# Gram strips of 64 channels, three load buffers in the first half, one pass for both means in the attention, and a product moved ahead of its statistics

## Chip and metric

The kernel runs on one core of a Trainium2 chip. The metric is the device time of one execution in microseconds; before the change its median is 2893.17 us over three runs (2892.83 to 2900.12). The core's engines each work through their own queue in order: PE (TensorE, matrix products; PEld are its weight loads), DVE (VectorE), ACT (ScalarE), POOL (GpSimd) and SP (SyncE, which here only issues DMAs). They meet at semaphores.

## The reference

The input x has the shape (16, 32, 128, 128), float32. Two layers follow each other, each a residual around a group norm and a block. The first is an attention over channels, the second a set of window-wise "FastKAN" blocks. Cut to what matters:

```python
def _gn(v, G=16, eps=1e-5):            # pairs of neighbouring channels
    g = v.reshape(B_, G, C_ // G, H_, W_)
    m = jnp.mean(g, axis=(2, 3, 4), keepdims=True)
    s = jnp.var(g, axis=(2, 3, 4), keepdims=True)
    return ((g - m) / jnp.sqrt(s + eps)).reshape(v.shape)

# layer 0: 8 heads; 8 images together form 256 channels, so there are two halves of the batch
q, k, v = Wq @ t, Wk @ t, Wv @ t                       # t = gn(x), 256 x 16384
attn = softmax(q_h @ k_h.T * 64 ** -0.5)               # 64 x 64 per head
x = x + Wout @ (attn.T-weighted v) + bout

# layer 1, on y = layernorm(windows of gn(x))
def _fastkan(x, ln_g, ln_b, ws, wb, bb):
    ln = _layernorm(x, ln_g, ln_b)
    basis = jnp.exp(-((ln[..., None] - GRID) / DENOM) ** 2)     # 8 grid points
    return flat(basis) @ ws.T + jax.nn.silu(x) @ wb.T + bb
z = fastkan_1(y over rows) + fastkan_2(y over columns) + fastkan_3(y over channels)
x = x + fastkan_4(z) + windows
```

Since queries and keys meet only summed over all 16384 pixels, layer 0 needs of x only the 256 x 256 matrix of its channel products (the Gram matrix) and the channel sums. From these the kernel builds one 256 x 256 matrix per half (`pt`), and layer 0 is then one product of that matrix with x.

## The kernel before

**Stages.** For each half of the batch (`bp` 0 and 1) the Gram loop runs over 16384 pixels: `gram_load` brings 2048 pixels of 256 channels in eight DMAs of 256 KB (four issued by SP, four by ACT) into one of two pairs of tiles (`ad` with `yy`, and two `u`); `gram_turn` turns 512 pixels at a time from channels to pixels on DVE (L653, two transposes a step, into one of two `R` tiles); `gram_sum` adds the products of a step on PE (L676). There are eight loads and 32 steps per half. A step has four blocks of 128 pixels. In a block, the upper triangle of the Gram matrix is made of eight matmuls, each for a strip of 32 channels: in the first bank (`k` = 0) for channels 0 to 127 against all channels from the strip on and a column of ones, in the second for channels 128 to 255. A float32 matmul stands in the profile as two records, each with its own weight load.

`attention(bp)` then turns the Gram matrix into `pt`. It subtracts the rank-one matrix of the channel means (`row_of`, `rank_one`), makes the whole matrix from the triangle with transpositions on PE (`gram_to`, giving the covariance `cov`), derives the group norm's variances, adds the rank-one matrix of the mean's deviations back and repeats `gram_to` scaled by the norm (`gc`). Then come the products with the key weights (L833), the similarity (L848), the softmax, and the products with output and value weights (L874, L883), which give `pt`. From `pt` and `cov` follow the statistics of the second group norm (L908 to L964), stored in `l0c`; after that the key `("layer0", bp)` is set.

Layer 1 works on 64 units of 1024 pixels by 128 channel rows. `layer0_norm` waits for `("layer0", bp)`, makes the product with `pt` (L999) into a PSUM tile of the kind `Y`, and ACT scales it with `l0c` (L1008). The rest of a unit runs through norms, a ladder of 14 long DVE instructions (L1163) and products on PE (L436). Units overlap.

**What sets the order.** All tasks are generators which ask for steps (`step(engine, us, tiles...)`). A planner (`Flow.run`) merges them into one order for each engine, from the costs in the text and the times at which tiles come free; an order of the steady pipeline is written out in `ORDER`, and takes hold once the second Gram sum is found. The engines then keep that order. Tiles of one kind are handed round: `Y` and `X` (PSUM) have two buffers each, `u` six, `ad_r`, `d` and `sd` one each. Until the last similarity, `attention` holds `ad_r`, where its query and key weights lie; `move_back` of a unit needs that tile.

At the start POOL issues 96 small DMAs for parameters (L304 to L308, L501 to L511) and then those of the attention's weights (L598 to L602). DVE prepares the parameters in `parameters`, between the Gram loop's transposes: L572 stands ahead of the transposes of step 20 of the first half, L576 and L577 ahead of those of step 21.

Of the kernel before, what the change touches and what calls it, by code (L numbers as in the profile page):

```python
# [12 lines left out]
ALU = mybir.AluOpType  # L13
# [6 lines left out]
P = 128  # L20
# [219 lines left out]
def conv_preact_kernel(  # L240
# [203 lines left out]
    def layers():  # L444
        with ExitStack() as es:
# [164 lines left out]
            def gram_load():  # L610


                for m in range(NBP * S // LOAD):
                    if m == 0:
                        ad, yy, u0, u1 = yield step("SP", 2.6, "ad", "yy", "u", "u", lag=-2.6)
                        flat4 = lambda t: t.rearrange("p l t w -> p (l t w)")
                        xs = [
                            [t.rearrange("p (g n) -> p g n", g=4) for t in pair]
                            for pair in ((flat4(ad), flat4(yy)), (u0, u1))
                        ]  # L620
                    else:
                        if m >= 2:
                            yield "get", ("turned", 4 * (m - 2) + 3)
                        yield step("SP", 2.6, lag=-2.6)
                    bp, j = divmod(m, S // LOAD)
                    for queue in (nc.sync, nc.scalar):
                        if queue is nc.scalar:
                            yield step("ACT", 2.6)
                        for r in (0, 1) if queue is nc.sync else (2, 3):
                            for k in range(KK):  # L630
                                at = j * LOAD + r * 512
                                queue.dma_start(
                                    out=xs[m % 2][k][32 * r : 32 * r + 32],
                                    in_=x_groups[bp, k, :, :, at : at + 512],
                                )
                    put(("xs", m), xs[m % 2], fl.moved(6.5, 2.6))

            def gram_turn():
# [6 lines left out]
                for m in range(NBP * STEPS):  # L645
                    xr = yield "get", ("xs", m // 4)
                    if m >= 2:
                        yield "get", ("summed", m - 2)
                    yield step("DVE", 1.3)
                    o = slice(128 * (m % 4), 128 * (m % 4) + 128)  # L650
                    for k in range(KK):
                        at = k * (P + 1)
                        nc.vector.transpose(  # L653
                            turned[m % 2][:, :, at : at + P].rearrange("p b (g c) -> p g b c", g=4), xr[k][:, :, o]
                        )
                    put(("turned", m), None)
                    put(("xT", m), turned[m % 2])

            def gram_sum():

                strips = [(0, q, 32 * q, 2 * P + 1) for q in range(4)]
                strips += [(1, q, P, P + 33 + 32 * q) for q in range(3, -1, -1)]
                for m in range(NBP * STEPS):
# [5 lines left out]
                    for b in range(4):  # L671
                        yield step("PE", 0.57, lag=0.0)
                        first, last = i == 0 and b == 0, i == STEPS - 1 and b == 3
                        for k, q, lo, hi in strips:
                            at = k * (P + 1) + 32 * q
                            MM(  # L676
                                g[32 * q : 32 * q + 32, k, lo:hi],
                                lhsT=t[:, b, at : at + 32],
                                rhs=t[:, b, lo:hi],
# [9 lines left out]
            def attention(bp):  # L689
                g_ = yield "get", ("gram", bp)  # L690
                wq, wk, wv_raw, wo, low, mid = yield "get", "projections"
                pt = pts[bp]
                rows = [low[0:1, 512 + i * 256 : 768 + i * 256] for i in range(2)]
                att = mid[:, 1536:1792].rearrange("p (h n) -> p h n", h=PAIRS)
                b_sb = low.rearrange("p (h n) -> p h n", h=PAIRS)
# [31 lines left out]

                def row_of(columns, to):

                    ps_, = yield step("PE", 0.65, "Y")  # L730
                    for k in range(KK):
                        MM(
                            ps_[0:1, 0, k * P : (k + 1) * P],
                            lhsT=columns[:, k : k + 1],
                            rhs=ident,
                            start=True,
                            stop=True,
                        )
                    yield step("DVE", 0.45)
                    nc.vector.tensor_copy(to, ps_[0:1, 0, 0 : KK * P])  # L740
                    give("Y")

                def rank_one(row, scaled, by):
                    yield step("DVE", 0.3)
                    TS(scaled, row, by, None, ALU.mult)
                    ps_, = yield step("PE", 0.9, "Y")
                    for k in range(KK):
                        MM(
                            ps_[:, k, k * P : KK * P],
                            lhsT=scaled[:, k * P : (k + 1) * P],  # L750
                            rhs=row[:, k * P : KK * P],
                            start=True,
                            stop=True,
                        )
                    yield step("DVE", 0.7)
                    for k in range(KK):
                        o = slice(k * P, KK * P)
                        TT(g[:, k, o], g[:, k, o], ps_[:, k, o], ALU.add)
                    give("Y")

                def gram_to(dst, r):

                    yield step("ACT", 0.3, lag=0.0)
                    nc.scalar.copy(parts[:, 2, :], g[:, 0, P : KK * P])
                    yield step("DVE", 0.6)
                    for k, mask in enumerate((upper, lower)):
                        TT(
                            parts[:, k, :].rearrange("p (q c) -> p q c", q=4),
                            g[:, k, k * P : (k + 1) * P].rearrange("p (q c) -> p q c", q=4),
                            mask.unsqueeze(2).to_broadcast([P, 4, 32]),  # L770
                            ALU.mult,
                        )
                    ps_, = yield step("PE", 0.9, "Y")
                    for k in range(KK):
                        to = ps_[:, k, 0:P]
                        MM(to, lhsT=parts[:, k, :], rhs=ident, start=True, stop=False)
                        MM(to, lhsT=ident, rhs=parts[:, k, :], start=False, stop=True)
                    MM(ps_[:, 1, P : 2 * P], lhsT=parts[:, 2, :], rhs=ident, start=True, stop=True)
                    scaled = lambda to, src, k: (
                        nc.vector.tensor_copy(to, src)  # L780
                        if r is None
                        else TS(to, src, r[:, k : k + 1], None, ALU.mult)
                    )
                    yield step("DVE", 1.0)
                    scaled(dst[:, 0, 0:P], ps_[:, 0, 0:P], 0)
                    scaled(dst[:, 0, P:], parts[:, 2, :], 0)
                    scaled(dst[:, 1, 0:P], ps_[:, 1, P : 2 * P], 1)
                    scaled(dst[:, 1, P:], ps_[:, 1, 0:P], 1)
                    give("Y")

                def averaged(matrix, columns, to):
# [14 lines left out]
                give("X", LAG)  # L806
                yield from row_of(mx, rows[0])
                yield from rank_one(rows[0], rows[1], -float(S))
                yield from gram_to(cov, None)


                var, dg, m, d = cols2(), cols2(), cols2(), cols2()
                yield from averaged(pair_n, mx, m)
                yield step("DVE", 1.9)
                for k in range(KK):
                    TT(own, cov[:, k, k * P : (k + 1) * P], ident, ALU.mult)
                    nc.vector.tensor_reduce(dg[:, k : k + 1], own, AX.X, ALU.add)
                TT(d, mx, m, ALU.subtract)
                TT(var, d, d, ALU.mult)
                STT(var, dg, 1.0 / S, var, ALU.mult, ALU.add)  # L820
                gvar = cols2()
                yield from averaged(pair_n, var, gvar)

                yield from row_of(d, rows[0])
                r, _ = yield from rsqrt(gvar)
                yield from rank_one(rows[0], rows[1], float(S))
                yield from gram_to(gc, r)

# [62 lines left out]
                for k in range(KK):  # L891
# [9 lines left out]
                    TT(mine, mine, perm, ALU.add)  # L901
                give("Y")


# [87 lines left out]
            def layer0_norm(n):  # L992
                bp, kk, j = units[n]
                yield "get", ("layer0", bp)
                xr = yield "get", ("x", n // 2)
                xh, xp = yield step("PE", 3.65, "xh", "Y")
                for u in range(2):
                    for k in range(KK):
# [6 lines left out]
                        )  # L1005
                used(("x", n // 2), "x", 2)
                yield step("ACT", 1.06)
                ACT(xh, flat(xp), AF.Identity, bias=l0col(bp, kk, C_XB), scale=l0col(bp, kk, C_R2))  # L1008
# [474 lines left out]
```

## Time and profile before

The profiled execution took 2896.12 us; its span, from the first to the last instruction, is 2894.3 us. All times in the profile are counted from the span's start.

| engine | busy us | share of the span | instructions |
|---|---|---|---|
| PE | 2747.0 | 95% | 48023 |
| PEld | 1085.6 | 38% | 48023 |
| DVE | 2689.1 | 93% | 1811 |
| ACT | 2514.8 | 87% | 2027 |
| POOL | 53.6 | 2% | 109 |

| event | at us |
|---|---|
| first Gram matmul (L676) | 17.1 |
| matmuls of step 20 of the first half | 80.4 |
| DVE clears PSUM for the second half (L669) | 118.6 |
| first product of layer 0 (L999) | 193.5 |
| last Gram matmul record | 235.5 |
| first ladder instruction (L1163) | 250.3 |
| similarity of the second attention (L848) | 302.1 to 305.3 |
| next ladder instruction after it | 324.5 |

A row of the stretches has the stretch (from:to) and its length, then for each engine its busy time and number of instructions, the clock granted to PE (1.00 is full), the share of time in which DMA engines were busy, and GB/s. A row of the waits names who waited for whom, the sum in us, the number of times and the longest. A piece of the chain of waits has its start, its length and the engine, tile and line. In a row of the timeline, start and length come first, then engine, line, operation, tiles and shapes, the number of instructions merged into the row, and in brackets the idle time before it with what ended it. The queue q8 carries instructions to the engine that runs most of them.

### The profile page before, as it was taken

The page shows a single profiled execution, that of the slowest core. Times are in us where ns is not written, and L with a number is a line of the kernel's source. Part 1 is how long each engine was busy: PE and PEld are TensorE (multiplying, and loading weights), DVE is VectorE, ACT ScalarE, POOL GpSimd, SP SyncE. Part 2 cuts the span into 40 slices and gives each one's busy share as a digit, 9 for nine tenths or more (in the row PEclk, how much of TensorE's full clock was granted, in tenths as well). Part 3 has the DMA queues.
Part 4 walks back from the last instruction along what each step waited for, and adds up shares of the span by engine and source line. Part 5 has one row for each costly group of instructions (what it writes and reads, how often), then busy time and mean ns, then how long its engine had stood idle before and what let it go on. Part 6 is the DMA issues. An engine that isn't in the chain of part 4 may idle for free.

```text
span 2894.3 us, 104845 instructions
## 1 busy us (share of the span) xinstructions
PE 2747.0 (95%) x48023; PEld 1085.6 (38%) x48023; DVE 2689.1 (93%) x1811; ACT 2514.8 (87%) x2027; POOL 53.6 (2%) x109
## 2 busy tenths in 40 slices
PE   5798899999999999999999999999999999999985
PEld 5774433333333333333333333333333333333321
DVE  4557699999999999999999999999999999999986
ACT  0018599999999999999999999999999999999973
POOL 6100000000000000000000000000000000000000
PEclk9999899999999999999999999999999999999987
DMA  7751233333333333333333333333333333333311
GB/s 193 187 157 52 67 101 107 116 113 96 106 105 110 114 115 102 112 101 115 113 103 95 109 106 116 114 109 105 107 108 115 107 95 113 100 113 113 103 54 36
DMA packets 206168, 311.31 MB, mean 108 GB/s; under 512 B 24480, under 2 KB 156064, under 8 KB 205728
## 3 DMA queue, kind: packets, MB, share of 16 engines
q1 hardware_dynamic: 192512, 285.29, 33.5%
q10 hardware_dynamic: 9504, 16.85, 2.2%
q8 instruction: 378, 6.19, 0.9%
q0 software_dynamic: 3712, 2.46, 0.4%
q14 instruction: 62, 0.51, 0.1%
HBM read 103.18 MB, written 67.11 MB: 59 GB/s over the span
## 4 chain that ended last, share of the span: by engine, by line
PE 63%; DVE 21%; issue 6%; ACT 5%; DMA 3%; SPq 1%; POOL 1%; DVEq 0%; ACTq 0%; POOLq 0%
PE X L436 25%; DVE u L1163 15%; PE X L1199 10%; PE Y L999 7%; PE Y L436 4%; PE Y L1013 4%; PE X L1318 4%; DVE yc L1134 3%; PE X L676 3%; PE Y L1117 2%; DVE yy L1051 2%; PE Y L976 2%; DMA col<-in_cols 1%; DMA sz<-in_w 1%; SPq L1235 1%
## 5 line engine op out<-in xcount | busy, mean ns | idle before, releaser
L1163 DVE SCALAR_TENSOR_TENSOR u<-R,u 128x2048 f32<-128x2048 f32 x910 | 2043.6, 2286 | 35.4 <-ACT u L1148 17.1
L436 PE MATMUL X<-u,wt_a 32*32 32x512 f32 x16384 | 663.4, 602 | 8.9 <-ACT u L1148 4.2
L436 PE MATMUL X<-u,wt_b 32*32 32x512 f32 x16896 | 637.9, 604 | 16.6 <-ACT u L1148 9.4
L436 PEld LDWEIGHTS X<-u,wt_a 32*32 32x32 f32 x16384 | 301.6, 103 | 287.5 <-issue 136.0
L436 PEld LDWEIGHTS X<-u,wt_b 32*32 32x32 f32 x16896 | 224.1, 103 | 384.0 <-issue 192.4
L1134 DVE TENSOR_TENSOR yc<-yc,Y 128x1024 f32<-128x1024 f32 x260 | 305.4, 1216 | 9.3 <-PE Y L1117 6.7
L1143 ACT ACTIVATE u<-yc,vec 128x2048 f32<-128x2048 f32 x130 | 258.5, 1989 | 30.9 <-DVE yc L1134 26.4
L999 PE MATMUL Y<-x,pt 128*128 128x512 f32 x512 | 236.8, 605 | 33.7 <-DVE yc L1134 33.7
L1109 ACT ACTIVATE yc<-Y 128x1024 f32<-128x1024 f32 x260 | 250.3, 1016 | 13.8 <-PE Y L436 13.8
L1151 ACT ACTIVATE R<-yc,vec 128x2048 f32<-128x2048 f32 x130 | 259.5, 1996 | 2.1 <-DVE u L1163 1.1
L1145 ACT ACTIVATE R<-yc,vec 128x2048 f32<-128x2048 f32 x130 | 258.8, 1990 | 0.0
L1112 ACT ACTIVATE u<-yc 128x2048 f32<-128x2048 f32 x130 | 247.7, 1905 | 3.7 <-DVE u L1163 3.0
L1148 ACT ACTIVATE u<-u 128x2048 f32<-128x2048 f32 x130 | 247.1, 1901 | 0.0
L676 PE MATMUL X<-R 128*32 128x257 f32 (+7 forms) x4096 | 150.2, 303 | 46.8 <-issue 26.3
L978 ACT ACTIVATE lr<-Y,vec 128x512 f32<-128x512 f32 (+1 forms) x194 | 131.5, 678 | 46.2 <-PE Y L976 41.9
L676 PEld LDWEIGHTS X<-R 128*32 128x32 f32 x4096 | 136.0, 115 | 66.3 <-issue 36.4
L999 PEld LDWEIGHTS Y<-x,pt 128*128 128x128 f32 x512 | 92.0, 189 | 182.6 <-issue 92.6
L976 PE MATMUL Y<-u,e 128*32 128x512 f32 x1040 | 139.6, 604 | 3.4 <-ACT u L1112 3.4
L1227 ACT ACTIVATE ad<-X,col 128x1024 f32<-128x1024 f32 x128 | 134.0, 1096 | 0.1
L1013 PE MATMUL Y<-xh,c 128*128 128x512 f32 x256 | 127.0, 618 | 1.3 <-DVE yc L1134 1.3
L979 ACT ACTIVATE lr<-lr 128x512 f32<-128x512 f32 (+1 forms) x194 | 122.3, 631 | 6.1
L1199 PE MATMUL X<-sd,silu_a 64*64 64x512 f32 x1024 | 124.7, 602 | 0.0
(202 smaller groups left out, 2486.5 us busy)
## 6 DMA issues: line engine op xcount, KB each, us to landing
xh<-xh SPq DMA_DIRECT2D x128, 512.0 KB
d<-yy SPq DMA_DIRECT2D x512, 128.0 KB
ad_r<-ad SPq DMA_DIRECT2D x512, 128.0 KB
x<-in_x SPq DMA_DIRECT2D x32, 1024.0 KB
out<-xh SPq DMA_DIRECT2D x256, 128.0 KB
u<-in_x SPq DMA_DIRECT2D x32, 256.0 KB
u<-in_x ACTq DMA_DIRECT2D x32, 256.0 KB
ad<-in_x SPq DMA_DIRECT2D x16, 256.0 KB
```

Source lines behind the costliest of these rows:

```text
L436: MM(dst(to, g_), lhsT=wt[32 * g_ : 32 * g_ + 32, :], rhs=rhs(g_, (to - turn[g_]) % 4), start=start, stop=stop,)
L676: MM(g[32 * q : 32 * q + 32, k, lo:hi], lhsT=t[:, b, at : at + 32], rhs=t[:, b, lo:hi], start=first, stop=last,)
L999: MM(xp[:, u, :], lhsT=pts[bp][:, k, kk * P : (kk + 1) * P], rhs=xr[:, k, u * 512 : (u + 1) * 512], start=k == 0, stop=k == KK - 1,)
L1109: ACT(v[:, i * RB : (i + 1) * RB], flat(yt[i]), AF.Identity)
L1112: ACT(sq, v, AF.Square)
L1134: TT(v[:, o], v[:, o], flat(rb[i]), ALU.mult)
L1143: ACT(u, v, AF.Square, bias=bq)
L1145: ACT(up, v, AF.Exp, bias=bp_, scale=2.0)
L1148: ACT(u, u, AF.Exp, scale=-1.0)
L1151: ACT(down, v, AF.Exp, bias=bn, scale=-2.0)
L1163: STT(t, by, BIG, tiles[at[way]], ALU.min, ALU.mult)
L1199: MM(dst(i, f), lhsT=wt(i)[o, o], rhs=rhs(i, o), start=False, stop=False)
```

## The change

In `gram_load`, a third pair of tiles (`d` with `sd`) takes part in the first half's loads, in turn with the two others; `gram_turn` gives it back after the last step of that half. In `gram_sum`, strips are 64 channels wide, four matmuls a block in place of eight. In `attention`, the rows of the channel means and of the mean's deviations are made together, the two rank-one matrices in one PSUM tile, the transposition is done once (for `cov`), and `gc` is the sum of `cov` and the second rank-one matrix, scaled afterwards; several copies go to ACT. `layer0_norm` waits for a new key `("matrix", bp)`, which is set when `pt` is there, makes its product, and waits for `("layer0", bp)` only ahead of the scaling on ACT. The helpers `row_of`, `rank_one` and `gram_to` go.

```diff
@@ gram_load
-                for m in range(NBP * S // LOAD):
+                half = S // LOAD
+                turn = [m % 3 if m < half else m % 2 for m in range(NBP * half)]
+                for m in range(NBP * half):
                     if m == 0:
-                        ad, yy, u0, u1 = yield step("SP", 2.6, "ad", "yy", "u", "u", lag=-2.6)
+                        ad, yy, u0, u1, d, sd = yield step("SP", 2.6, "ad", "yy", "u", "u", "d", "sd", lag=-2.6)
...
-                            for pair in ((flat4(ad), flat4(yy)), (u0, u1))
+                            for pair in ((flat4(ad), flat4(yy)), (u0, u1), (flat4(d), flat4(sd)))
...
-                        if m >= 2:
-                            yield "get", ("turned", 4 * (m - 2) + 3)
+                        old = [i for i in range(m) if turn[i] == turn[m]]
+                        if old:
+                            yield "get", ("turned", 4 * old[-1] + 3)
...
@@ gram_turn
+                    if m == STEPS - 1:
+                        give("d")
+                        give("sd")
@@ gram_sum
-                strips = [(0, q, 32 * q, 2 * P + 1) for q in range(4)]
-                strips += [(1, q, P, P + 33 + 32 * q) for q in range(3, -1, -1)]
+                strips = [(0, q, 64 * q, 2 * P + 1) for q in range(2)]
+                strips += [(1, q, P, P + 65 + 64 * q) for q in range(1, -1, -1)]
...
-                            at = k * (P + 1) + 32 * q
+                            at = k * (P + 1) + 64 * q
                             MM(
-                                g[32 * q : 32 * q + 32, k, lo:hi],
-                                lhsT=t[:, b, at : at + 32],
+                                g[64 * q : 64 * q + 64, k, lo:hi],
+                                lhsT=t[:, b, at : at + 64],
                                 rhs=t[:, b, lo:hi],
@@ attention
-                yield from row_of(mx, rows[0])
-                yield from rank_one(rows[0], rows[1], -float(S))
-                yield from gram_to(cov, None)
                 var, dg, m, d = cols2(), cols2(), cols2(), cols2()
                 yield from averaged(pair_n, mx, m)
-                yield step("DVE", 1.9)
+                yield step("DVE", 0.2)
+                TT(d, mx, m, ALU.subtract)
+                ps_, = yield step("PE", 1.0, "Y")
+                for i, columns in enumerate((mx, d)):
+                    for k in range(KK):
+                        MM(ps_[0:1, i, k * P : (k + 1) * P], lhsT=columns[:, k : k + 1], rhs=ident, ...)
+                yield step("ACT", 0.55, lag=0.0)
+                for i in range(2):
+                    nc.scalar.copy(rows[i], ps_[0:1, i, 0 : KK * P])
+                yield step("DVE", 0.8)
+                for i in range(2):
+                    TS(scaled[i], ps_[0:1, i, 0 : KK * P], float(S) if i else -float(S), None, ALU.mult)
+                give("Y")
+                ps_, = yield step("PE", 1.7, "Y")
+                for i in range(2):
+                    for k in range(KK):
+                        o = slice(0 if i else k * P, KK * P)
+                        MM(ps_[:, k, i * KK * P + o.start : (i + 1) * KK * P],
+                           lhsT=scaled[i][:, k * P : (k + 1) * P], rhs=rows[i][:, o], ...)
+                yield step("DVE", 0.7)
+                for k in range(KK):
+                    o = slice(k * P, KK * P)
+                    TT(g[:, k, o], g[:, k, o], ps_[:, k, o], ALU.add)
+                yield step("ACT", 0.9, lag=0.0)
+                nc.scalar.copy(parts[:, 2, :], g[:, 0, P : KK * P])
+                nc.scalar.copy(gc, ps_[:, :, KK * P :])
+                give("Y", LAG)
...
+                yield step("ACT", 0.5, lag=0.0)
+                nc.scalar.copy(cov[:, 1, 0:P], ps_[:, 1, P : 2 * P])
+                nc.scalar.copy(cov[:, 0, P:], parts[:, 2, :])
+                yield step("DVE", 2.3)
+                nc.vector.tensor_copy(cov[:, 0, 0:P], ps_[:, 0, 0:P])
+                nc.vector.tensor_copy(cov[:, 1, P:], ps_[:, 1, 0:P])
...
-                yield from row_of(d, rows[0])
+                TT(gc, gc, cov, ALU.add)
+                give("Y")
                 r, _ = yield from rsqrt(gvar)
-                yield from rank_one(rows[0], rows[1], float(S))
-                yield from gram_to(gc, r)
+                yield step("DVE", 0.5)
+                for k in range(KK):
+                    TS(gc[:, k, :], gc[:, k, :], r[:, k : k + 1], None, ALU.mult)
...
                     TT(mine, mine, perm, ALU.add)
                 give("Y")
+                put(("matrix", bp), None, LAG)
@@ layer0_norm
-                yield "get", ("layer0", bp)
+                yield "get", ("matrix", bp)
                 xr = yield "get", ("x", n // 2)
                 xh, xp = yield step("PE", 3.65, "xh", "Y")
...
                 used(("x", n // 2), "x", 2)
+                yield "get", ("layer0", bp)
                 yield step("ACT", 1.06)
```

## The prediction

> **What bounds the kernel now.** I read the stretches first, cut where the work changes: start, first half of the Gram loop up to a stop of VectorE, its rest, second half, start of the layer-1 pipeline, steady pipeline.
>
> ```profile
> core 0: us, PE busy (x) PEld busy (x) DVE busy (x) ACT busy (x) POOL busy (x), PEclk, DMA share, GB/s
> 17.10:80.40 63.30, 47.88 (x1287) 43.88 (x1288) 34.19 (x89) 0.00 (x0) 42.18 (x85) 0.92 0.73 180
> 80.40:118.70 38.30, 29.02 (x768) 26.68 (x768) 18.03 (x29) 0.00 (x0) 2.49 (x3) 0.87 0.82 216
> 118.70:235.60 116.90, 111.13 (x2320) 88.47 (x2312) 64.11 (x150) 23.29 (x30) 0.00 (x0) 0.97 0.56 149
> 235.60:305.30 69.70, 57.82 (x741) 22.66 (x736) 59.25 (x71) 52.80 (x44) 0.00 (x0) 0.98 0.08 24
> 400.00:2800.00 2400.00, 2355.46 (x40512) 852.25 (x40504) 2365.28 (x1324) 2328.65 (x1867) 0.00 (x0) 1.00 0.36 107
> ```
>
> From 400 us on, PE, DVE and ACT are all busy 97 to 99%. The change touches none of that work, and in the instruction order of the two programs each engine runs the same steps there. So the question is how much earlier the pipeline starts; a microsecond gained before 400 us is a microsecond of the span. PE sets the second Gram half (111.1 of 116.9 us busy). In the first half it idles 15.4 + 9.3 us, and the waits of PE from 17.2 to 118.7 us name the cause (17.1 us of the second row is the start):
>
> ```profile
> PE X L676 <- issue: 22.5, 9, 4.2
> PE X L676 <- DVE R L653: 19.3, 4, 17.1
> ```
>
> "Issue" is a wait for nothing the profile shows. The chain of waits shows two limits there, one after the other:
>
> ```profile
> 65.23 7.30 DMA sz<-in_w
> ...
> 75.80 4.55 DMA sz<-in_w
> 80.49 0.25 DVE sz L576
> ...
> 81.56 0.64 DVE R L653
> ...
> 85.22 4.20 PE X L676 x75
> 89.42 4.19 issue
> ...
> 100.63 8.18 PE X L676 x152
> 108.81 3.11 issue
> ```
>
> Up to 81.5 us the chain is POOL's row of small parameter loads: VectorE takes its queue in order, and the parameter steps (L572 ahead of the transposes of step 20, L576 ahead of those of step 21) wait for the last of them. After it, PE with holes of 3 to 4 us.
>
> **The holes are late instructions.** PE runs 48023 matmul and as many weight-load instructions; queue q8 moved 6.19 MB in 378 packets, which is 64 B for each and 256 in a packet. One Gram step (512 pixels, 32 matmuls of two records) is 128 instructions, so a packet lasts two steps, 4.4 us. Asked in slices of 1 us, q8 moved a packet in those that begin at 45, 58, 71, 82 and 109 us, each at the end of a 2 MB burst of x, and PE resumed at 48.5, 60.9, 73.7, 85.2 and 111.9, some 2.5 us later each time. From the start of one packet's work to that of the next took 7 to 8.4 us there (85.22 to 93.61 the longest), against 4.4 us of work.
>
> The Trainium skill, "Runtime: NRT & Kernel Launch", section "Instruction fetch mechanics", agrees on 256 instructions, but calls the fetch hidden by the rate of issue, with 2048 instructions held for PE. By that rule the holes are something else, and the term of 9.3 us below would be nothing. The rows of q8 decide against it.
>
> **Strips of 64.** Removed: 16 of the 32 matmuls of a step, 64 of its 128 instructions. Columns: the four 32-wide strips stream 1160 columns side by side in four column strips, 290 each; the two 64-wide ones 644 in two, 322 each.
>
> ```profile
> 66.19 2.18 PE L676 MATMUL X<-R 128*32 128x257 f32 x64
> 193.50 3.70 PE L999 MATMUL Y<-x,pt 128*128 128x512 f32 x8
> 157.79 1.20 PE L848 MATMUL Y<-att,ad_r 128*64 128x64 f32 x32
> ```
>
> Now 2.18 us a step. L999 streams 8 x 512 columns in 3.65 us (its piece in the chain of waits; 3.70 with its tail), 0.89 ns a column; 322 x 2 records x 4 blocks at that rate is 2.30 us, the lower bound. Scaling the present step by 322/290 gives 2.42, the upper. L848 has 64-wide strips and shows that two overlap: 32 x 64 columns one by one would be 1.82 us, it took 1.20. I take 2.35: +0.17 a step. A packet now lasts 9.4 us, over the longest fetch seen (8.4), so I take the holes as gone.
>
> **Three load buffers.** No load is added. The first half's eight loads go out up to one buffer earlier; SyncE and ScalarE issue the same DMAs in the same places, and ScalarE has no other work until 118 us. VectorE's waits for x loads after the first one sum to 2.6 us up to 118 us (rows of the waits: 2.2 and 0.4), so the direct gain is nothing. What it costs: the bursts close up, and POOL's parameter loads run among them. From 36.5 to 76.8 us POOL issued 56, about 1.2 per us inside a burst and 1.75 between. PE without holes does step 18 by 17.1 + 18 x 2.35 = 59 us and then stands on the same in-order parameter steps; loads stand with it, as their buffers do not come free, and POOL regains the quiet rate. From 37 to 58 us at 1.2 per us, 25 are issued; then one more burst of 8 us (10) and 21 at 1.75 end at 78, and with 4.5 of landing the last is usable at 82.5, against 80.4 to 81.5 now: +1. Bounds: 96 issues of 0.5 us never waiting end near 50 + 4 us, and then PE itself sets the end (17.1 + 32 x 2.35 = 92, 26 us earlier than 118.7); all at the busy rate, 56/1.2 from 37 on, end at 84 + 8, 10 later. I take +1, as both ends correct themselves.
>
> So the first half's saving of 20 steps dies in the wait for parameters. What counts is its last 12 steps: now 38.3 us, 29.0 busy (26.2 at 2.18, the rest at a granted clock of 0.87 after each hole) and 9.3 idle. After: 12 x 2.35 = 28.2, with 1.5 for one slow restart 29.7. First half: 29.7 - 38.3 + 1 = -7.6 us.
>
> **Second half.** PE is the limit: 32 x 0.17 = +5.4; issue waits there were 3.9 us in 3 holes, taken as gone; attention's PE work see next, -1.5. Together 0, bounds -3 to +6.
>
> **Attention in one pass.** Removed for each half: the second row-of-columns, rank-one and transposition passes. Three of the eleven PE trips between the Gram sum and the similarity go. PE work: one transposition set (1.6 us) less, one 256-column rank-one product more (0.1 to 0.2), -1.5. Added: ACT copies (0.3 to 0.5 us each; ACT idles 94 of 117 us in the second half), one DVE add, one scaling. In the first attention the trips lie under Gram steps on PE, so only the 1.5 counts. The second runs among the pipeline's first unit; from 235.6 to the similarity (L848, 302 to 305.3) PE idles 11.9 us. Three of eleven trips are 3 us of it, with 1.5 of work 4.5; I take -4. Bounds 0 (the idle time belongs to the pipeline filling) and -13 (all of it). What follows does not shrink: the similarity still releases ad_r, whose move (5.1 us of issues plus 4 of landing) and the softmax still hold PE and DVE until some 19 us later, as now (305.3 to 324.5).
>
> **Product before the group norm's statistics.** L999 of unit 0 (3.65 us) moves about six Gram steps forward in PE's order. PE is saturated, so its sum is unchanged; it holds one of two Y buffers while the statistics chain, serial anyway, uses the other. ACT's L1008 still waits for l0c. Next product and transposes behind it stand at the same Gram steps as before. Nothing; if PE had been idle there, 3.65 us would be won.
>
> **Sum.** -7.6 + 0 - 4 = -11.6. The profiled execution took 2896.12 us (span 2894.3); the median is 2893.17. So 2893.2 - 11.6 = 2881.6, said as 2881.
>
> **Rivals.**
> 1. *Parameters stop binding* (POOL done by 65 to 70 us): -26 instead of -7.6 at most; halfway, -17 - 4: 2872, at best 2863. For: the quiet gaps were real. Against: 96 issues and the waits of the chain.
> 2. *Same*: a step of 2.42 (+0.07 x 44 = +3), parameters 4 us later, pipeline start gains nothing: -11.6 + 3 + 3 + 4 = -1.6, 2891. For: L848 has 36 ns a record, more than L676's 34. Against: these must fall together.
> 3. *Slower*: 64-wide strips cost much more because the two column strips do not run side by side as four do, at L676 in the saturated stretch. Price 44 steps x (c - 2.35). Decides at c = 2.61 (no gain) and is beyond 0.3% slower at 2.82; wholly one by one, c = 4.6, +99 - 12: 2980; a quarter of that overlap lost, 2.9, gives +24 - 12: 2906, which I take as its time. For: no row shows strips of this shape with unequal widths. Against: L848.
> 4. *The fetch is not it*: holes stay (9.3 + 3.9): 2894.8. It falls into rivals 2 and 3.
>
> **Chances.** Forecast (2872 to 2886) 0.45, rival 1 0.15, rivals 2 and 4 (2886 to 2899) 0.25, rival 3 0.15. 0.3% is 8.7 us, about what a measurement here can tell from none: below 2884.5 lie 0.43 of the forecast and rival 1, 0.58; above 2901.9 rival 3 and a tail, 0.17; the rest 0.25. For 8 in 10 I cut 2863 below and 2896 above.
>
> **What would show it.** Right: no issue holes of 3 us in the Gram stretch, half of q8's packets there; PE waiting for R (DVE) some 15 to 20 us ahead of step 20 or 21, and that step at 81 to 83 us; the X memset of the second half near 111 instead of 118.6; second half as long as before; L848 of the second attention some 65 us after the last Gram matmul. Wrong: steps over 2.6 us, holes that stay, or a start of step 21 far from 82 us.

## The result, and the profile after

The changed kernel takes 2882.26 us (median of seven runs, 2881.65 to 2886.40), the kernel before 2893.66 us (2892.83 to 2904.04) beside it, so the medians differ by 11.4 us. The ratio of their fast runs is 0.9947, with a 95% interval of 0.9936 to 0.9957, which would be 12 to 19 us. The two agree only roughly; the gain is best taken as 11 to 15 us. The profiled execution took 2885.47 us; its span is 2883.7 us against 2894.3.

The total came out as forecast (2881, that is -11.6 us). The parts did not. The account below takes marks from the timelines of the two profiled executions; a unit is marked by DVE's product in its norm (`yy<-xc,Y`), and the 17th ladder instruction is the first one behind the second attention's similarity before, at 324.5 us.

| stretch | before, us | after, us | difference | predicted |
|---|---|---|---|---|
| start to first Gram matmul | 17.1 | 17.2 | 0.0 | 0 |
| to the matmuls of step 20 | 63.3 | 72.5 | +9.3 | +1 |
| last 12 steps, to the clearing of PSUM | 38.2 | 28.5 | -9.6 | -8.6 |
| second half, to the last Gram record's end | 117.1 | 116.0 | -1.1 | 0 |
| from there to the 17th ladder instruction | 88.8 | 79.5 | -9.4 | -4 |
| to the norm of unit 4 | 64.8 | 68.7 | +4.0 | 0 |
| unit 4 to unit 63 | 2341.6 | 2338.4 | -3.2 | 0 |
| to the end | 163.5 | 162.9 | -0.6 | 0 |

Each column is one execution, and the first half scatters. Two kernels below, with only the attention or only the key changed, run the same instructions there in the same order as the kernel before; they started step 20 at 84.7 and 84.2 us, not 80.4, and their first half took 99.1 and 97.1 us, not 101.4. Against them the +9.3 would be 5 to 6 and the -9.6 only -2 to -3.

The first half's own gain was lost again; the attention gave 5.4 us net; and 3 us more appear in the steady pipeline, where nothing was changed. All fourteen profiled executions here, whose DVE and ACT run the same steps there, lie between 2338.4 and 2341.7 us, so those 3 us are scatter of which this pair shows the two ends.

The waits of PE in the first half of the kernel after (17.2 to 118.5 us: who waited for whom, sum, times, longest):

```profile
PE X L683 <- DVE R L657: 38.2, 7, 17.2
```

The "issue" row, 22.5 us before, is gone: PE now waits for the transposes alone (17.2 us of the row is the start, so 21.0). Also gone are half of q8's packets between 17 and 118 us, first before, then after (packets, MB, share):

```profile
q8 instruction: 15, 0.25, 1.1%
q8 instruction: 8, 0.13, 0.6%
```

The stretches of the kernel after, cut where the work changes (first Gram matmul, step 20, clearing, last Gram matmul, similarity):

```profile
core 0: us, PE busy (x) PEld busy (x) DVE busy (x) ACT busy (x) POOL busy (x), PEclk, DMA share, GB/s
17.10:89.70 72.60, 51.49 (x643) 47.73 (x643) 34.24 (x91) 0.00 (x0) 41.72 (x85) 0.89 0.94 208
89.70:118.50 28.80, 28.78 (x383) 27.38 (x383) 18.07 (x29) 0.00 (x0) 3.02 (x4) 0.91 0.61 153
118.50:234.20 115.70, 114.39 (x1287) 92.08 (x1284) 63.73 (x142) 27.44 (x35) 0.00 (x0) 0.99 0.57 150
234.20:295.40 61.20, 53.61 (x724) 20.33 (x722) 51.99 (x60) 49.48 (x46) 0.00 (x0) 0.97 0.09 27
```

From step 20 on PE is full (28.78 of 28.80). Ahead of it PE idles 21.1 us, 5.7 more than before. The chain of waits of the kernel after says for what:

```profile
57.29 7.42 DMA sz<-in_w
...
64.99 6.71 DMA sz<-in_w
...
77.22 7.29 DMA wt_b<-in_w
...
85.83 1.80 DMA sz<-in_w
...
88.17 0.70 DVE R L657
...
89.72 26.78 PE X L683 x261
...
118.25 0.92 DVE X L676
```

It is the same row of parameter loads as before, only that its last load goes out at 86 us and not at 76. What DVE waited for in that half, on the same columns:

```profile
DVE wt_b L572 <- DMA sz<-in_w: 11.4, 1, 11.4
DVE sz L550 <- DMA sz<-in_w: 10.7, 2, 8.4
```

Each of these waits stands ahead of transposes in DVE's order, and PE stands behind those. The step itself is read off the transposes that wait for PE's `R`, in the saturated stretch of the kernel after:

```profile
107.72 1.52 DVE L657 STREAM_TRANSPOSE R<-u 128x512 f32<-128x512 f32 x2 [0.67 <-PE X L683]
109.92 1.53 DVE L657 STREAM_TRANSPOSE R<-u 128x512 f32<-128x512 f32 x2 [0.68 <-PE X L683]
112.12 1.53 DVE L657 STREAM_TRANSPOSE R<-u 128x512 f32<-128x512 f32 x2 [0.67 <-PE X L683]
```

One step every 2.20 us, against 2.18 with strips of 32, as long as PE has only Gram steps to do. In the second half other products lie between the steps, and there the Gram records alone kept PE busy for 3 us more than before, as these two rows show (stretch, length, PE's busy time on the products of `R`, clock, DMA share, GB/s; before, then after):

```profile
118.57:235.66 117.09, 74.16 (x2059) 0.97 0.56 149
118.25:234.25 116.00, 77.22 (x1032) 0.99 0.57 151
```

Over the five executions with strips of 32 that time is 72.0 to 74.2 us; in the kernel with the strips of 64 alone it is 78.0. So a step costs 0.1 to 0.2 us more there.

Back to the first half: its last twelve steps took 28.5 us; 12 x 2.20 is 26.4, and 2.1 went to the restart: PE began at a granted clock of 0.52, as two stretches of 5 us show.

```profile
90.00:95.00 5.00, 5.00 (x42) 4.55 (x42) 2.67 (x7) 0.00 (x0) 1.45 (x3) 0.52 1.01 215
95.00:100.00 5.00, 5.00 (x79) 4.86 (x75) 3.05 (x5) 0.00 (x0) 1.22 (x1) 1.00 0.51 101
```

The second attention, from the timeline of the kernel after:

```profile
294.16 1.20 PE L851 MATMUL Y<-att,ad_r 128*64 128x64 f32 x32 [0.70 <-DVE yc L1139]
...
298.15 2.28 DVE L1168 SCALAR_TENSOR_TENSOR u<-R,u 128x2048 f32<-128x2048 f32 x1
313.71 2.28 DVE L1168 SCALAR_TENSOR_TENSOR u<-R,u 128x2048 f32<-128x2048 f32 x1
318.07 9.28 DVE L1168 SCALAR_TENSOR_TENSOR u<-R,u 128x2048 f32<-128x2048 f32 x4 [0.47 <-PE X L436]
```

The similarity ends 61.1 us after the last Gram record (69.6 before), and the 17th ladder instruction starts at 313.71, 18.3 us behind it (19.2 before). Then 4.0 us of these 9.4 are given back: from that instruction to the norm of unit 4 DVE was busy 59.3 of 64.8 us before and 60.1 of 68.7 after. It now waits for ACT, which waits for PE's products of a unit; the waits of DVE in the kernel after from 313.7 to 382.4 us begin so:

```profile
DVE u L1168 <- ACT yc L1114: 3.4, 1, 3.4
```

### The profile page after: what moved, and what is told of

Its sections match the earlier page's. It is cut to its first block, busy times and chain, and to the rows that moved or that the text cites. A ratio compares the mean times of both kernels' runs of the same rounds, so it can differ in the third digit from the quotient of the medians.

```text
span 2883.7 us, 100690 instructions
## 1 busy us (share of the span) xinstructions
PE 2748.3 (95%) x45955; PEld 1092.4 (38%) x45955; DVE 2685.2 (93%) x1793; ACT 2518.4 (87%) x2035; POOL 53.8 (2%) x109
## 4 chain that ended last, share of the span: by engine, by line
PE 64%; DVE 21%; issue 6%; DMA 4%; ACT 3%; SPq 1%; DVEq 0%; POOL 0%; ACTq 0%; POOLq 0%
PE X L436 25%; DVE u L1168 15%; PE X L1204 10%; PE Y L1003 8%; PE Y L1018 4%; PE Y L436 4%; PE X L1323 4%; PE X L683 3%; DVE yc L1139 3%; PE Y L980 2%; PE Y L1122 2%; DVE yy L1056 2%; DMA sz<-in_w 1%; DMA col<-in_cols 1%; SPq L1240 1%
## 5 line engine op out<-in xcount | busy, mean ns | idle before, releaser
L683 PE MATMUL X<-R 128*64 128x193 f32 (+3 forms) x2048 | 156.7, 313 | 39.0 <-DVE R L657 38.2
L683 PEld LDWEIGHTS X<-R 128*64 128x64 f32 x2048 | 145.1, 142 | 56.7 <-DVE R L657 40.8
```

The lines of the kernel that those rows point to most:

```text
L683: MM(g[64 * q : 64 * q + 64, k, lo:hi], lhsT=t[:, b, at : at + 64], rhs=t[:, b, lo:hi], start=first, stop=last,)
```

## Experiments

Each kernel ran against the kernel before on the same chip. The interval of a ratio reaches 0.1 to 0.2% to either side, 3 to 5 us; the marks in a profile are finer, but are one execution. Two stretches are used: the first half, from the first Gram matmul to DVE's clearing of PSUM (101.4 us before, 101.1 after), and what follows it, from the clearing to the norm of unit 4 (270.7 before, 264.2 after). The kernel before took 2895 to 2897 us beside these runs, so ratios are compared, not times.

### The four parts one by one

Strips alone, in the kernel before:

```diff
-                strips = [(0, q, 32 * q, 2 * P + 1) for q in range(4)]
-                strips += [(1, q, P, P + 33 + 32 * q) for q in range(3, -1, -1)]
+                strips = [(0, q, 64 * q, 2 * P + 1) for q in range(2)]
+                strips += [(1, q, P, P + 65 + 64 * q) for q in range(1, -1, -1)]
...
```

> Before with 64-channel strips alone: two load buffers, attention and product as before. Theory A (late instruction packets make the holes): PE has no issue wait of 3 us left in the Gram stretch; as the third buffer is not there to crowd POOL's loads, step 20 still starts at 80 to 83 us, the second half starts near 109 instead of 118.6, and the time is 2880 to 2886. Theory B (the holes are something else, the gain came from the attention): holes stay, second half starts at 117 to 119, time 2891 to 2895.

2884.37 us, ratio 0.9953 [0.9942, 0.9965]. The waits of PE in its first half:

```profile
PE X L676 <- DVE R L653: 29.4, 3, 16.8
```

No wait for "issue" is left, the first half takes 90.9 us, and what follows it is unchanged (271.5). Step 20 started at 78.7 us, a little ahead of the 80 to 83 expected. So the strips alone bring 10.5 us in the first half, more than the 7.6 that the prediction gave to the whole change there, and far more than the whole change got.

The third load buffer alone:

```diff
+                turn = [m % 3 if m < half else m % 2 for m in range(NBP * half)]
...
-                            for pair in ((flat4(ad), flat4(yy)), (u0, u1))
+                            for pair in ((flat4(ad), flat4(yy)), (u0, u1), (flat4(d), flat4(sd)))
```

> Before with three load buffers in the first half alone. Theory A (closed-up loads slow POOL's parameter loads, and the parameters gate step 20): step 20 starts at 86 to 91 us instead of 80.4, holes of PE stay in the steps before it, the second half starts at 117 to 123, time 2892 to 2898. Theory B (the buffer costs nothing and the parameters moved late for another reason): step 20 at 80 to 83 us, time 2885 to 2893.

2898.24 us, ratio 1.0001 [0.9993, 1.001]. The waits of PE in its first half:

```profile
PE X L683 <- DVE R L657: 27.3, 3, 17.8
PE X L683 <- issue: 15.6, 6, 4.5
```

The holes stay, and step 20 starts at 87.1 us, as theory A said; but the second half starts at 114.5 us, ahead of its range, since PE had one hole of 1.8 us in the steps behind it. Over the whole kernel the buffer alone neither helps nor harms.

The attention in one pass alone (the change's edits in `attention`, without the new key):

```diff
-                yield from row_of(mx, rows[0])
-                yield from rank_one(rows[0], rows[1], -float(S))
-                yield from gram_to(cov, None)
...
+                for i, columns in enumerate((mx, d)):
...
-                yield from gram_to(gc, r)
```

> Before with the one-pass attention alone. Theory A (fewer PE trips bring the second similarity, L848, forward among the pipeline's first unit): first half as before (second half starts at 118 to 119.5), similarity ends 8 to 10 us earlier after the last Gram matmul than the 70 us of before, of which about 4 are given back by the next unit; time 2883 to 2888. Theory B (only its 1.5 us of PE work counts): 2890 to 2892.5.

2885.69 us, ratio 0.996 [0.9947, 0.9973]. The holes stay here too (15.3 us in 7), and what follows the first half takes 267.1 us, 3.6 less than before. The similarity ended 65.0 us after the last Gram record, 4.7 earlier than before and not the 8 to 10 expected. The first half, in which the same instructions run as before, took 99.1 us instead of 101.4; that is scatter, here and in the next run.

The key alone:

```diff
+                put(("matrix", bp), None, LAG)
...
-                yield "get", ("layer0", bp)
+                yield "get", ("matrix", bp)
...
+                yield "get", ("layer0", bp)
                 yield step("ACT", 1.06)
```

> Before with the product of layer 0 waiting for the matrix alone, not for the norm's statistics. Theory A (PE is saturated there, a step moved within its queue changes nothing): last Gram matmul at 234.5 to 236.5 us, time 2891 to 2895. Theory B (the product was on the path): 3 to 4 us less, 2889 to 2890.5.

2890.49 us, ratio 0.9976 [0.9964, 0.9988]; at 2893 for the kernel before that is 2886, below the range of either theory. Its profile gives 4.3 us to the first half, whose instructions up to there are those of the kernel before, and 2.3 to what follows. This could not tell whether the moved product is worth anything; the last experiment below asks again.

### What the third buffer does beside the strips

The changed kernel with two load buffers, as in the kernel before (the second diff above taken back):

> The changed kernel with two load buffers in the first half as before (strips, attention and product as changed). Theory A (the third buffer crowds POOL's parameter loads and gives the strips' gain back): step 20 starts at 79 to 83 us instead of 89.7, the second half starts at 107 to 110 instead of 118.3, the rest as in the changed kernel; ratio to before 0.990 to 0.993, 2.5 to 10 us below the changed kernel. Theory B (the third buffer does not matter): second half at 116 to 119, ratio 0.994 to 0.996.

2871.77 us, ratio 0.9913 [0.9899, 0.9926]: faster than the whole change, whose interval is 0.9936 to 0.9957. Its first half takes 90.1 us. The stretches of this kernel up to the wait for parameters:

```profile
17.00:37.00 20.00, 19.70 (x250) 18.91 (x252) 11.52 (x17) 0.00 (x0) 13.41 (x27) 1.00 0.83 210
37.00:57.00 20.00, 20.00 (x280) 18.48 (x278) 14.56 (x41) 0.00 (x0) 12.95 (x27) 1.00 0.95 244
57.00:65.00 8.00, 6.12 (x90) 5.73 (x84) 5.25 (x29) 0.00 (x0) 4.78 (x10) 1.00 0.57 136
```

And the same stretches of the changed kernel, with three:

```profile
17.00:37.00 20.00, 19.82 (x246) 18.89 (x247) 10.69 (x16) 0.00 (x0) 10.52 (x21) 1.00 1.08 229
37.00:57.00 20.00, 19.07 (x261) 17.59 (x259) 14.27 (x40) 0.00 (x0) 9.46 (x20) 1.00 1.07 231
57.00:65.00 8.00, 5.77 (x81) 5.23 (x79) 4.51 (x17) 0.00 (x0) 4.01 (x9) 1.00 1.07 239
```

PE does nearly the same in both. The column to read is POOL's number: 27 + 27 + 10 = 64 issues with two buffers, 21 + 20 + 9 = 50 with three. With three the DMA engines have no gap (share 1.07 to 1.08 throughout), so that POOL's small loads land later (the 4.5 KB ones after 7.3 us in the median, 6.3 with two) and POOL, which waits for some of them, issues about one per us instead of 1.3. The 14 issues that are missing cost some 10 us behind: the last load of the row goes out at 75 us with two buffers, at 86 with three. In ratios, strips, attention and key alone add up to 1.1% less time, the three together with two buffers give 0.87%, and with the third buffer 0.53% is left.

### The wait for parameters itself

The changed kernel (three buffers), with all parameter steps of DVE that stood between the Gram loop's transposes held until the first half's last step is turned:

```diff
+                yield "get", ("turned", STEPS - 1)
                 yield step("DVE", 0.6)
                 nc.vector.memset(back_t, 0.0)
```

> The changed kernel with the parameter steps of VectorE and PE moved behind the first half's Gram steps. Theory A (the parameters are the gate of the first half): PE runs all 32 steps without a wait for R over 1 us, the second half starts at 89 to 93 us instead of 118.3; attention may then wait for its own weights until 100; ratio 0.982 to 0.988. Theory B (something else, as the loads of x, holds the first half): second half at 105 or later, ratio over 0.990.

2862.32 us, ratio 0.9881 [0.9864, 0.9898]. Its first half as one stretch:

```profile
16.80:91.20 74.40, 73.53 (x1024) 70.00 (x1024) 46.22 (x75) 0.27 (x1) 41.44 (x84) 1.00 1.03 236
```

74.4 us for 32 steps, PE busy for 73.5 of them at the full clock. The parameters end 17 us later than in the changed kernel (107.5 against 90.3 us), and nobody waits for them there: what follows the first half takes 266.1 us, about as after.

The same edit with two buffers:

> As the run with late parameters, but with two load buffers. Theory A (a load takes about 8 us of the 8.8 that four steps last, so two buffers leave small waits for R at each load, which the third hides): second half starts at 93 to 100 us, ratio 0.984 to 0.990, behind the three buffers. Theory B (the third buffer only takes bandwidth from the parameters): second half as early or earlier than with three.

2866.09 us, ratio 0.9888 [0.9872, 0.9904]; first half 78.9 us. The second half starts at 95.7 us, in theory A's range, but not by its mechanism. PE runs all 32 steps in 72.5 us with no wait for `R`; the time goes behind them, where DVE waits for the second half's first load, and its clearing of PSUM (L670) stands behind those transposes:

```profile
16.75 72.45 PE L677 MATMUL X<-R 128*64 128x257 f32 x1024 [16.75 <-DVE R L654]
...
90.51 0.71 DVE L654 STREAM_TRANSPOSE R<-ad 128x512 f32<-128x512 f32 x1 [3.81 <-DMA ad<-in_x]
94.17 0.71 DVE L654 STREAM_TRANSPOSE R<-yy 128x512 f32<-128x512 f32 x1 [2.94 <-DMA yy<-in_x]
```

Once the parameters are out of the way, the third buffer does no harm, and at most brings the 3 to 4.5 us that the stretch up to the clearing is shorter with it; the totals' intervals overlap.

### Number of instructions, or their shape

The changed kernel with strips of 32 (the first diff taken back):

> The changed kernel with strips of 32 channels. Theory A (late instructions): issue waits of 3 to 4.5 us are back in the Gram stretch, before and after the parameters; step 20 again at 85 to 91 us, second half starts at 116 to 123; ratio 0.996 to 0.999. Theory B (strips do not matter): as the changed kernel, 0.994 to 0.995.

2886.8 us, ratio 0.9968 [0.9958, 0.9979]; first half 97.7 us. The waits of PE in it:

```profile
PE X L683 <- DVE R L657: 25.1, 3, 18.3
PE X L683 <- issue: 14.1, 7, 3.7
```

The holes are back. This does not tell the number of instructions from the width, so the next kernel keeps the strips of 64 and fills up the number:

```diff
                                 rhs=t[:, b, lo:hi],
...
+                            if bp == 0:
+                                MM(
+                                    spare[64 * q : 64 * q + 64, k, 0:1],
+                                    lhsT=t[:, b, at : at + 64],
+                                    rhs=t[:, b, 0:1],
...
```

> The changed kernel, but in the first half each strip's matmul is followed by one more of a single column into a second X tile, whose result nobody reads: 128 instructions a step again, with the 64-wide strips kept. Theory A (the holes come from the number of instructions: a packet of 256 lasts two steps): issue waits of PE of 1.5 to 4.5 us return in the first half, 8 to 20 us in 5 to 9 waits, and the packets of q8 there double. Theory B (a 32-wide shape makes the holes, not the number): no issue wait over 1 us, as in the changed kernel. The time says little by itself, since each extra matmul costs work on PE: step between 2.3 and 3.3 us, total 2880 to 2905 on the scale where the kernel before has 2893.

2911.17 us, ratio 1.0052 [1.0037, 1.0067]. The waits of PE in its first half, which is now PE's own 113.7 us long (3.55 a step):

```profile
PE X L685 <- DVE R L657: 17.5, 1, 17.5
PE X L693 <- issue: 3.9, 3, 2.5
PE X L685 <- issue: 1.4, 2, 1.2
```

Waits for "issue" return, 14 packets of q8 are back between 17 and 118 us, and the longest wait, 2.5 us, is too long for the theory of the shape. The three longest end each 2.5 to 2.8 us after a packet of q8 started (at 29.96, 38.98 and 98.65 us), as in the kernel before:

```profile
32.79 0.16 PE L693 MATMUL X<-R 128*64 128x1 f32 x1 [1.24 <-issue]
41.73 0.17 PE L693 MATMUL X<-R 128*64 128x1 f32 x1 [2.49 <-issue]
101.17 0.33 PE L685 MATMUL X<-R 128*64 128x65 f32 x2 [1.16 <-issue]
```

But the sum is 5.3 us, not the 8 to 20 expected: the extra matmuls make a step so long (the 2.3 to 3.3 expected are exceeded too) that a packet lasts 7.1 us, which most fetches stay under. So the number decides, together with the time that a packet lasts: 4.4 us a packet gives 14 to 22 us of holes, 7.1 us gives 5, and 8.8 us (four steps of 2.20) none.

### The next limit, and the product

On top of late parameters, the first load of layer 1's `x`, 1 MB that SP issues ahead of the Gram loads, is held until step 7 is turned:

```diff
+                if n == 0:
+                    yield "get", ("turned", 7)
                 bp, kk, j = units[n]
                 xr, = yield step("SP", 1.6, "x")
```

> Late parameters as before, and the first load of layer 1's x (unit 0, 1 MB, issued ahead of the Gram loads) is held until step 7 of the first half is turned. Theory A (the first Gram load waits behind that megabyte on the DMA engines): first Gram matmul 2.5 to 5 us earlier than 16.8, everything after it as much earlier, ratio 0.9865 to 0.9875 against 0.988 with late parameters alone. Theory B (the start is set by latency and code, not by bytes): first Gram matmul within 1 us of 16.8, ratio as with late parameters alone.

2860.39 us, ratio 0.9877 [0.9862, 0.9892]. PE's timeline in its first half:

```profile
14.79 19.63 PE L684 MATMUL X<-R 128*64 128x257 f32 x256 [14.79 <-DVE R L658]
34.63 9.01 PE L684 MATMUL X<-R 128*64 128x257 f32 x128 [0.22 <-DVE R L658]
43.89 9.01 PE L684 MATMUL X<-R 128*64 128x257 f32 x128 [0.24 <-DVE R L658]
55.51 37.07 PE L684 MATMUL X<-R 128*64 128x257 f32 x512 [2.61 <-DVE R L658]
```

The start moves 2.0 us forward, between the two theories, though clear of the 16.8 to 18.3 us of all other executions here: the megabyte costs something, less than said. At 53 us 2.6 us are lost again, as DVE waits 2.6 us for a load of x there; the first half takes 79.0 us and ends 2.6 us later than in the first execution of late parameters alone, 1.2 later than in the one below. So the gain was nothing. That the first half is by now about as long as its loads (DMA share 1.00 to 1.03) would explain it; no run tested that.

Late parameters once more, beside it:

> The kernel with late parameters once more, beside the one above on the same chip. Ratio 0.987 to 0.989; first Gram matmul at 16.8, clearing of PSUM for the second half at 91 to 92 us.

2860.82 us, ratio 0.9877 [0.986, 0.9893]; clearing at 92.6 us, what follows 268.7. Between this execution and the first of the same kernel that stretch differs by 2.7 us.

Late parameters, with layer 0's product again behind the statistics:

```diff
-                put(("matrix", bp), None, LAG)
...
-                yield "get", ("matrix", bp)
+                yield "get", ("layer0", bp)
                 xr = yield "get", ("x", n // 2)
...
-                yield "get", ("layer0", bp)
                 yield step("ACT", 1.06)
```

> Late parameters as before, but layer 0's product again behind the statistics of the second group norm, as in the kernel before. Theory A (the moved product is worth nothing): ratio as with late parameters, 0.987 to 0.989, and from the clearing of PSUM for the second half to the norm of unit 4 as long as there, 266 to 269 us. Theory B (it is worth the 2 to 7 us that the key alone seemed to bring): ratio 0.9895 to 0.991, that stretch 269 to 273 us.

2862.21 us, ratio 0.9886 [0.9868, 0.9903]; what follows the first half takes 267.4 us, between the 266.1 and 268.7 us of the same kernel with the product moved. The stretch speaks for no gain. The ratios' intervals, some 5 us to either side, would not rule out the 2 to 7 us either; what the key alone seemed to bring is not seen again here, and not excluded.

The fastest versions are those with late parameters, 1.2% below the kernel before and some 0.7% below the changed one.

## Why the prediction held, and where it did not

**The holes and the fetch.** Right. Strips alone take them away, fillers bring some of them back with the shape kept. Rival 4 falls with that. The Trainium skill, "Runtime: NRT & Kernel Launch", section "Instruction fetch mechanics", calls the fetch of the next 256 instructions hidden by the rate of issue; here it was not, as long as a packet lasted 4.4 us and the x loads ran beside it.

**The step.** Taken at 2.35 us with a lower bound of 2.30; it is 2.20. The bound was wrong where PE has only Gram steps: it took 0.89 ns a column from L999, and 2.20 us over 2 x 4 x 322 columns are 0.85. With half as many instructions the step hardly grew there, +0.02 where +0.17 was said. Among the other products of the second half it grew by 0.1 to 0.2, as said. That two strips of 64 run side by side well enough was right, and rival 3 falls.

**The wait for parameters.** This is the term that was mis-sized: +1 us was said, +9.3 measured, near the upper bound of 10 (5 to 6 against the two other executions of the same first half). The step that failed is the sentence that PE "then stands on the same in-order parameter steps; loads stand with it" and "POOL regains the quiet rate" from 66 us or so. The slower rate began earlier, not at 37 us but with the Gram loop (21 issues from 17 to 37 us against 25 before), and it lasted longer, as a third buffer lets one more load of 2 MB go out (issued from 57.7 to 64.5 us): the DMA engines were full until 70 us. The rate inside the bursts, 1.2 per us, was also read too high, about 1.0 with no gaps. "Both ends correct themselves" held for neither.

**The last twelve steps.** -9.6 against -8.6: 12 x (2.35 - 2.20) = 1.8 us better in the step, 0.6 worse in the restart (2.1 for 1.5).

**The second half.** 0 was said, -1.1 came, as the terms changed about as said in sum: the Gram records added 3.1 us (+5.4 said), the transpositions that went took off 3.1 (-1.5 said), and PE's idle time fell by 4.5, from 5.8 to 1.3, with the waits for "issue" (3.9) gone. What was not said: records of the units behind worth 3.9 us moved ahead of the last Gram record.

**Attention.** -4 against -5.4 net (-9.4 and +4.0). Over the runs with the one pass, what follows the first half took 261 to 269 us (275 with the fillers), without it 268 to 274; on average 265.6 without the fillers, and 271.1. The working was less good than its sum: PE's idle time up to the similarity fell by 4.3 us and its work there by 4.2, where 3 and 1.5 were said; "what follows does not shrink" held up to the next ladder (18.3 for 19.2 us), but the pipeline behind it gave 4.0 us back to a wait for products, which was not foreseen. PE's records tell what the 4.2 us are: its transpositions there went from 28 records to 18 (8.0 to 5.0 us), and six records of other units (3.7 us) moved ahead of the last Gram record, while some others took longer.

**The moved product.** Nothing was said, and nothing is seen beside late parameters, within some 5 us.

**The third buffer.** "The direct gain is nothing" was right as long as the parameters bind; its cost beside the strips is the 10 us that the wait for parameters took. So the sum was right by luck, by three errors that cancel in this pair of executions: 8.3 us too little for the parameters; 3.5 us too much for the last twelve steps (1.0), the second half (1.1) and the attention with what it gave back (1.4); and 3.8 us by which the two executions differ behind unit 4 without a cause in the change. That leaves the 1.0 us between -11.6 and the -10.6 of the two spans. With the scatter of the first half, the size of the first of them is known to some 4 us, its sign and cause from the experiments.

**Rival 1**, that the parameters stop binding, was priced at 2863 at best. It did not happen by itself, but it is what late parameters make: first half 74.4 us, 27 less than before, and a ratio of 0.9881, 2859 us where the kernel before has 2893.

Of the signs named, these came: no holes, half the packets, PE's wait for `R` of 15 to 20 us (21), the second half as long. These did not: step 20 at 81 to 83 us (89.7), the clearing near 111 (118.25), the similarity 65 us after the last Gram record (60 to 61).

## What to carry to other kernels

Where a stream of short matmuls shows waits for "issue" while big loads run, count the instructions that one fetch brings and the time they last; here fewer and larger instructions cured it. Before bulk loads get another buffer, look who else's small loads go through the same DMA engines, and what stands behind them in an in-order queue. And a stage with two limits one after the other yields only what the second leaves: here one line that moved the parameters' steps was worth more than the whole change.

## What the runs showed of the hardware

- Around PE's idle time in the kernel after, the granted clock in the five stretches of 5 us from 70 to 95 us is 0.59, 0.50, 0.84, 0.50 and 0.52, and 1.00 again from 95 us, some 5 us after work resumed; the last stop cost about 2.1 us beyond its own length.
- Small loads issued by POOL between bulk loads fell from 1.3 to 1.0 per us when the last gaps between the bulk loads were closed (DMA share 0.57 to 0.95 against 1.07 and 1.08).
- Two column strips of 64 with 322 columns each took 2.20 us where Gram steps follow each other, four of 32 with 290 each 2.18; among other products the Gram records of 32 steps took 77.2 us and more against 72.0 to 74.2. Why is open: no run separated a fixed cost of each matmul from the cost of its columns.
- PE resumed some 2.5 to 2.8 us after a packet of q8 started, in the kernel before (45.9 to 48.5 us) as with the fillers (39.0 to 41.7).
